# Loading image 1's first group-norm tile and the second layer's weights within the planned first steps of a conv/attention kernel

## Chip, cores, metric

One core of one Trainium2 chip. The metric is the device time of one execution in microseconds (us). Ratios are the mean time of one kernel's fast runs over that of the other's of the same rounds on the same chip, so they are not quite the ratio of the medians quoted beside them; the profiled execution stands outside the rounds.

## The reference, cut to what matters

`x` is four images of 64x64 positions and 96 channels. The first layer works on `_gn(x)`, a group norm whose mean and variance need a whole image before its first position can be normalised:

```python
def _gn(v, G=32, eps=1e-5):
    g = v.reshape(B_, H_, W_, G, C_ // G)
    m = jnp.mean(g, axis=(1, 2, 4), keepdims=True)
    s = jnp.var(g, axis=(1, 2, 4), keepdims=True)
    return ((g - m) / jnp.sqrt(s + eps)).reshape(v.shape)

def step(h, ins):                     # a scan over the 4096 positions of an image
    h_new = d * (A_t * h) + d * (B_t * u_t[..., None])
    y = g_t * jnp.sum(C_t * h_new, axis=-1)
```

A, B, C and d, u, g are projections of the normalised x. The second layer (linear attention and a quantised FFN) uses ten weight and bias arrays that are not needed before the first layer has got some way.

## The kernel before: the parts concerned

The sequence is cut into 32 chunks of 512 positions, 8 for each image, and a chunk into 12 steps; in step s, tile s (one of 12 parts of the state) is scanned. The engines run their instructions in the order in which the program writes them (in the trace the gx load, which waits for nothing, is issued at 59.12 us, just after a read-back that had waited 2.7 us). There are two ways of writing them:

- the first six steps come out of a small **list scheduler** (`Plan`). Each job has an engine, a cost, and jobs it comes after; the scheduler picks the job that can start first by its own estimate, calls its function, and so fixes the order;
- all later work hangs on step numbers: `at(step, fn)`. What is hung on steps below 6 is written right after the planned part.

```python
def load_gx(b, i):
    t = gxt[b, i] = sb("gx", [P, J, C], F32, f"gx_{b}_{i}")
    nc.sync.dma_start(t, gx_v[b, i])

def load_late():                       # ten loads, cut
    nc.sync.dma_start(w_o[0:C, :], w_out)
    ...
    nc.sync.dma_start(b2_sb, b2.partition_broadcast(P))

class GroupNorm:                       # sums for the images 1 to 3, on TensorE and ScalarE
    def first(self):
        self.transpose(0, "M", "gc")   # four transposes of gx[b, 0] on TensorE
        t = small.tile([C, 1], F32, tag="gc", name=f"gc_{self.b}", bufs=2)
        nc.scalar.activation(self.ps, self.ps, AF.Copy, accum_out=t)
        ...

def group_norm(b, s0):
    ...
    if b == 1:
        when = [8, 15, 22, 29, 36, 43, 50, 57]
    at(when[0] - 7, load_gx, b, 0)     # step 1: written after the planned part
    at(when[0] - 2, make)              # step 6: GroupNorm(b).first()

def planned_start():
    ...
    a = job("SP", 0.5, second.write, after=[a], late=3.4)   # d, d*u of chunk 1 to DRAM
    job("SP", 1.8, second.read, after=[a])                  # and back, spread over 128 partitions (rep)
    ...
    plan.run(stay_awake)               # stay_awake: a filler matmul in planned gaps of TensorE
    return second

second = planned_start()
at(7, load_late)
```

SyncE (SP in the code and in the profile) issues nearly all loads and stores, in program order; an issue that has to wait holds up all behind it.

## Time and profile before

| | kernel before |
|---|---|
| time, median of 3 runs | 1226.73 us (1226.67 to 1226.94) |
| profiled span | 1224.3 us |
| TensorE / VectorE / POOL / ScalarE busy | 95 / 92 / 85 / 66% |
| longest single wait of TensorE | 9.5 us, for gx of image 1 |

In the lines of the timelines the first column is the start in us from the span's start, the second the duration; a bracket at the end tells how long the engine was idle before and what ended that. The clock in the views by stage is the share of TensorE's full clock that was granted: 1.00 is all of it (called warm below), and well under that is called cold.

### The profile page before, as it was taken

The page shows a single profiled execution, that of the slowest core. Times are in us where ns is not written, and L with a number is a line of the kernel's source. Part 1 is how long each engine was busy: PE and PEld are TensorE (multiplying, and loading weights), DVE is VectorE, ACT ScalarE, POOL GpSimd, SP SyncE. Part 2 cuts the span into 40 slices and gives each one's busy share as a digit, 9 for nine tenths or more (in the row PEclk, how much of TensorE's full clock was granted, in tenths as well). Part 3 has the DMA queues.
Part 4 walks back from the last instruction along what each step waited for, and adds up shares of the span by engine and source line. Part 5 has one row for each costly group of instructions (what it writes and reads, how often), then busy time and mean ns, then how long its engine had stood idle before and what let it go on. Part 6 is the DMA issues. An engine that isn't in the chain of part 4 may idle for free. (4 is left out here: it accounts for less than half of the span.)

```text
span 1224.3 us, 19361 instructions
## 1 busy us (share of the span) xinstructions
PE 1163.5 (95%) x5965; PEld 880.7 (72%) x5965; DVE 1130.5 (92%) x2103; ACT 808.6 (66%) x1808; POOL 1037.5 (85%) x1183
## 2 busy tenths in 40 slices
PE   6879999999999999899999999999999999999985
PEld 5666777777777777677777777677777777777663
DVE  6869999999999999799999999899999999999884
ACT  3546555655555677677777777777677677767474
POOL 5768878998888898899998898999999899989654
PEclk8989999999999999999999999999999999999999
DMA  7476667667777776766787778577866677667221
GB/s 181 97 146 149 149 144 163 153 155 154 160 158 164 174 157 133 175 158 154 161 175 159 151 159 184 128 158 154 179 150 159 152 172 158 151 144 162 64 67 39
DMA packets 104289, 182.14 MB, mean 149 GB/s; under 512 B 42637, under 2 KB 50769, under 8 KB 104186
## 3 DMA queue, kind: packets, MB, share of 16 engines
q1 hardware_dynamic: 90060, 106.96, 36.1%
q0 software_dynamic: 13536, 73.93, 30.0%
q8 instruction: 47, 0.77, 0.3%
q14 instruction: 56, 0.46, 0.1%
q10 hardware_dynamic: 590, 0.02, 0.0%
HBM read 69.12 MB, written 24.77 MB: 77 GB/s over the span
## 5 line engine op out<-in xcount | busy, mean ns | idle before, releaser
L751 POOL TENSOR_TENSOR bu<-bu,rep 128x512 f32<-128x512 f32 x384 | 560.9, 1504 | 11.7 <-ACT state L777 6.5
L748 ACT ACTIVATE bu<-Bps,b_bac 128x512 f32<-128x512 f32 x384 | 264.1, 688 | 287.7 <-PE Bps L244 265.7
L767 DVE TENSOR_TENSOR_SCAN h<-Aps,state,bu 128x512 f32<-128x512 f32 x336 | 426.4, 1269 | 12.7 <-POOL bu L751 3.5
L760 DVE SCALAR_TENSOR_TENSOR Aps<-Aps,b_bac,rep 128x512 f32<-128x512 f32 x384 | 282.4, 735 | 37.5 <-PE Aps L244 37.0
L244 PE MATMUL Bps<-xs,w 128*128 128x512 f32 x768 | 268.0, 430 | 3.3 <-ACT bu L748 3.2
L244 PE MATMUL Aps<-xs,w 128*128 128x512 f32 x768 | 249.1, 405 | 11.2 <-DVE h L767 10.1
L800 POOL TENSOR_TENSOR ch<-ch,h 128x512 f32<-128x512 f32 x128 | 195.0, 1523 | 13.6 <-ACT ch L797 13.3
L244 PEld LDWEIGHTS Aps<-xs,w 128*128 128x128 f32 x768 | 138.3, 188 | 67.3 <-DVE h L767 39.2
L244 PEld LDWEIGHTS Bps<-xs,w 128*128 128x128 f32 x768 | 129.3, 190 | 45.9 <-issue 25.2
L244 PE MATMUL Aps<-xl,w 128*128 128x512 f32 x384 | 152.1, 396 | 0.0
L244 PE MATMUL Bps<-xl,w 128*128 128x512 f32 x384 | 151.8, 395 | 0.0
L244 PE MATMUL Dps<-xs,w 128*128 128x512 f32 x384 | 120.9, 396 | 0.0
L244 PE MATMUL Cps<-xs,w 128*128 128x512 f32 x384 | 120.6, 395 | 0.0
L806 POOL DMA_DIRECT2D ch<-ch x94 | 89.8, 955 | 16.5 <-DMA ch<-ch 13.6
L791 DVE SCALAR_TENSOR_TENSOR ch<-Cps,b_bac,h 128x512 f32<-128x512 f32 x128 | 95.0, 742 | 0.5 <-PE Cps L244 0.5
L791 DVE SCALAR_TENSOR_TENSOR ch<-Dps,b_bac,h 128x512 f32<-128x512 f32 x128 | 94.7, 740 | 0.3 <-PE Dps L244 0.2
L244 PEld LDWEIGHTS Bps<-xl,w 128*128 128x128 f32 x384 | 72.5, 189 | 17.5
L244 PEld LDWEIGHTS Dps<-xs,w 128*128 128x128 f32 x384 | 72.4, 188 | 17.6
L244 PEld LDWEIGHTS Aps<-xl,w 128*128 128x128 f32 x384 | 72.3, 188 | 17.6
L244 PEld LDWEIGHTS Cps<-xs,w 128*128 128x128 f32 x384 | 72.1, 188 | 17.5
L244 PE MATMUL Dps<-xl,w 128*128 128x512 f32 x192 | 75.7, 394 | 0.0
L244 PE MATMUL Cps<-xl,w 128*128 128x512 f32 x192 | 75.7, 394 | 0.0
(196 smaller groups left out, 2086.4 us busy)
## 6 DMA issues: line engine op xcount, KB each, us to landing
ch<-ch POOLq DMA_DIRECT2D x94, 768.0 KB, 6.5
rep<-ddd SPq DMA_DIRECT2D x124, 384.0 KB, 5.8
ddd<-dd SPq DMA_DIRECT2D x31, 384.0 KB, 3.0
xl<-lo SPq DMA_DIRECT2D x62, 128.0 KB, 2.4
x<-in_x_dram SPq DMA_DIRECT2D x32, 192.0 KB, 3.0
xatd<-xat SPq DMA_DIRECT2D x32, 192.0 KB, 3.1
xal<-xatd SPq DMA_DIRECT2D x32, 192.0 KB, 4.7
out_dram<-o SPq DMA_DIRECT2D x32, 192.0 KB, 2.8
```

What stands on the lines that cost most here:

```text
L244: nc.tensor.matmul(ps, lhsT=wt[:, n], rhs=mv, start=(n == 0), stop=(n == 2))
L748: nc.scalar.activation(self.bu, self.b_ps, AF.Identity, bias=self.bias(0))
L751: nc.gpsimd.tensor_tensor(self.bu, self.bu, rep[self.b, self.i][:, 1, self.cg], ALU.mult)
L760: nc.vector.scalar_tensor_tensor(self.a_ps, self.a_ps, self.bias(1), rep[self.b, self.i][:, 0, self.cg], ALU.add, ALU.mult,)
L767: nc.vector.tensor_tensor_scan(self.h, self.a_ps, self.bu, 0.0 if self.i == 0 else state[self.sh, self.cg], ALU.mult, ALU.add,)
L791: nc.vector.scalar_tensor_tensor(self.slot(), self.c_ps, self.bias(2), self.h, ALU.add, ALU.mult)
L800: nc.gpsimd.tensor_tensor(self.ch, self.ch, self.h, ALU.mult)
L806: nc.gpsimd.dma_start(chs[g, 0], chs.pop((g, sh)), accum_op=ALU.add)
```

## The change

The intent: both loads depend on nothing, so they can be jobs of the planned start. `land("free0", 34.0)` is a job of no engine that ends at planned time 34.0, so the gx load is placed once SyncE is free after that, and the ten late weights after 37.0.

```diff
         when = [s0 + SUMS + NT * n for n in range(NCH)]
         if b == 1:
             when = [8, 15, 22, 29, 36, 43, 50, 57]
-        at(when[0] - 7, load_gx, b, 0)
+        if b > 1:
+            at(when[0] - 7, load_gx, b, 0)
         at(when[0] - 2, make)
@@
         job("SP", 1.8, second.read, after=[a])
+        plan.rank = 4
+        job("SP", 0.5, load_gx, 1, 0, after=[land("free0", 34.0)])
+        job("SP", 4.0, load_late, after=[land("free1", 37.0)])
@@
     second = planned_start()
 
-    at(7, load_late)
```

## The prediction

> **What bounds the kernel now.** I read five views in this order: the page (engine shares), the waits of TensorE over the whole span, the waits of the DMA queue, the timelines of SyncE and TensorE around the wait found, and busy time by stage. The page says that the body is bound by work, with TensorE first and VectorE close behind it:
>
> ```profile
> PE 1163.5 (95%) x5965; PEld 880.7 (72%) x5965; DVE 1130.5 (92%) x2103; ACT 808.6 (66%) x1808; POOL 1037.5 (85%) x1183
> ```
>
> So an isolated TensorE stall early in the kernel costs its length, unless later slack swallows it, and five idle per cent of 1224.3 us are about 61 us. The TensorE waits show one single item that stands out:
>
> ```profile
> PE Aps L244 <- DVE h L767: 10.1, 26, 1.4
> PE gc_ps L481 <- DMA gx<-in_x_dram: 9.5, 1, 9.5
> PE gx_ps L481 <- DMA x<-in_x_dram: 4.8, 3, 3.7
> ```
>
> Columns: total us, times, longest us. The second line is one wait of 9.5 us, for the very tile that the change moves. The SyncE timeline (start us, duration us) shows why that tile comes late:
>
> ```profile
> 39.19 0.59 SPq L238 DMA_DIRECT2D w<-w  x1
> 47.01 0.57 SPq L632 DMA_DIRECT2D xs<-lo  x1
> ...
> 53.97 0.34 SPq L681 DMA_DIRECT2D ddd<-dd  x1
> 57.04 2.04 SPq L688 DMA_DIRECT2D rep<-ddd  x4
> 59.12 0.44 SPq L112 DMA_DIRECT2D gx<-in_x_dram  x1
> 59.61 0.43 SPq L217 DMA_DIRECT2D w_o<-in_L_conv_W_out_dram  x1
> ```
>
> The gx load depends on nothing, but it is written after the whole planned start, so it sits in SyncE's in-order queue behind the write of dd (waits for VectorE until 53.97) and its read-back (waits for that write until 57.04), and behind 4 x 384 KB of read-back in the DMA engines. The queue is idle from 39.78 to 47.01. On TensorE:
>
> ```profile
> 57.99 0.40 PE L244 MATMUL Cps<-xl,w 128*128 128x512 f32 x1
> 67.91 1.09 PE L481 MATMUL gc_ps<-ident,gx 128*96 128x128 f32 x4 [9.53 <-DMA gx<-in_x_dram]
> 68.65 1.20 PE L244 MATMUL Bps<-xs,w 128*128 128x512 f32 x2
> ```
>
> 9.53 us idle, then matmuls at about twice their usual duration. By stage (length, then busy us of PE, PEld, DVE, ACT, POOL; granted clock, DMA share, GB/s):
>
> ```profile
> 40.00:46.00 6.00, 5.89 (x27) 4.05 (x26) 5.69 (x7) 3.32 (x6) 3.88 (x3) 1.00 0.11 26
> 58.00:62.00 4.00, 0.38 (x2) 0.00 (x0) 1.95 (x3) 0.00 (x0) 3.26 (x5) 0.97 1.04 223
> 62.00:68.00 6.00, 0.09 (x1) 0.09 (x2) 0.00 (x0) 0.00 (x0) 0.00 (x0) 0.50 0.89 178
> 68.00:72.00 4.00, 4.00 (x12) 3.29 (x13) 0.40 (x1) 2.88 (x9) 1.33 (x2) 0.50 0.33 86
> ```
>
> From 62 to 68 no compute engine does anything to speak of: this is a stall of the whole core, not of TensorE alone. In 40 to 46, where the load would go, the DMA engines are nearly empty.
>
> **What the Trainium skill says.** (1) "TensorE: Matmul & The Clock Gate", Part 1 (What's actually happening): after an idle window of about 3.4 us TensorE falls to half its clock, and gets it back after some 3.4 us of sustained work. The trace agrees: 0.50 granted in 62 to 68 and still in 68 to 72. So the stall is paid twice. (2) "DMA: Bandwidth & Descriptors", Anatomy of one DMA: DMA engines do not wait on semaphores; a wait happens on the issuing sequencer before dispatch. The trace agrees: gx has no dependency, yet is issued at 59.12, just after a read-back that waited 2.7 us for its write. (3) Same page, Queues, rings and completion order: descriptors of one queue are consumed in ring order on each engine. The trace agrees roughly: gx, 192 KB, took 8.7 us behind the read-back, against 3.4 us for the quickest gx load of the same stretch.
>
> **The change, part by part.** It adds no instruction and removes none; it moves eleven issues (one gx, ten late weights) up SyncE's order.
>
> Where they land: I took the list schedule of the kernel before as written. It gives SyncE its last weight copy at planned time 31.38 to 32.38, then nothing until the write of dd at 48.18; the split of the second tile (which issues xs and xl) is planned at 40.94. A job released at 34 and one released at 37 that takes 4.0 therefore fall after all fourteen weight copies and before xs/xl. They have no successors and are on SyncE alone, so the order on the compute engines does not move.
>
> In real time the last copy ends at 39.78. gx is then issued at about 39.85 and lands at about 43 to 44 (3.4 us), some 14 us before TensorE wants it at 58.38. The ten late issues last 3.25 us in the timeline before (0.43, 0.33, 0.32, 0.23, 0.32, 0.23, 0.40, 0.32, 0.31, 0.36), with some 0.06 between them about 3.9 us: 40.3 to 44.2. VectorE has lo ready for xs only at 47.0, so the issue time is free. Their bytes (gx 192 KB, weights 36+108+36+144+144+48 KB, in all about 0.7 MB) at some 200 GB/s take 3.6 us and fall into the stretch that moved 26 GB/s. They should be gone by about 46 to 47.
>
> What goes away:
> - TensorE's wait: 67.91 - 9.53 = 58.38, so 9.53 us.
> - The cold clock. From 67.91 to 72.35 (start of the B matmuls after D) TensorE does four transposes and three groups of three matmuls. In the warm part of the same timeline a group takes 0.70 (72.35 to 73.04, 73.04 to 73.74) and four transposes 0.35 (74.44 to 74.79): 3 x 0.70 + 0.35 = 2.45 instead of 4.44. That is 2.0 us.
> - Sum: 11.5 us. Cross-check on VectorE: it idles 11.54 us before its next a_mul at 71.60, and would now start that at about 60.3, when the warm A group is done; 11.3 us.
>
> The ten late weights being early brings nothing by itself: their first user is at step 20, and no wait on them is in the list.
>
> What is given back: in the old stall the read-back of rep landed unseen. The SyncE timeline shows this: each late issue after 61 starts about 2 us after the last (61.15, 63.22, 65.14, 67.18), each released by a piece of rep, so the last piece landed at about 67.1. Tile 12 is its first user. Its multiply on POOL ran at 77.28; 11.3 earlier is 66.0. Without the 0.38 MB that shared the wire, rep would end about 1.8 us earlier (65.3); but POOL's first accumulating gather (768 KB, issued at 71.89) now comes at about 62.6 (POOL ends its two multiplies at 61.35, then one of 1.28), into the tail of rep. Halving the rate from about 63.5 puts rep at 67 to 68.5 and the gather at about 70. POOL would then wait 1 to 2 us for rep and 1 to 3 us before the second gather. Scan 12, at about 72.3, and a_mul 12, at about 70.3, come later than that, and POOL has 6.8 us of slack in the 37 us after 72. I book 0.5 us of net loss. 11.5 - 0.5 = 11.0 gives 1226.73 - 11.0 = 1215.7, a gain of 0.9%.
>
> **Rivals.**
> (a) *The read-back becomes the new wait.* Rep or the gathers land later than I estimate, and tile 12 stalls VectorE and TensorE by 2 to 4 us, some of it with a cold clock again. For it: the DMA engines are full (1.04) exactly there, and the work that used to fall in the quiet now falls on top. Against: 2 us and more of margin at a_mul 12. It would make 1218 to 1220.
> (b) *The gain is given back later*, since POOL, or a DMA-bound stage downstream, set the pace and the old stall only let it catch up. For: POOL is 85% busy, and there is a 2.8 us wait of TensorE for xl at 497. Against: TensorE has no wait over 0.7 us for 400 us after 72, and all that feeds it is issued by engines that move up with it. It would make 1220 to 1226.
> (c) *Early loads hurt the start*: late weights delay xs/xl, whose user at 50.85 has only some 0.3 us of margin (the last xl copy starts at 48.27 and takes 2.3). For: a tight margin. Against: an empty wire from 42 on. It costs 1 us at most: 1216.7.
> (d) *Luck in the phase of DMA*: the wait at 497 vanishes or grows, plus or minus 2.5.
>
> **Range and chances.** The centre is the mechanism with a small loss. The low end, 1213.2, is the full 11.5 and half of (d); the high end, 1219.0, is most of (a). A gain over 2% would take 24.5 us, more than twice what this stall holds; a loss over 2% would need a new stall of 36 us net of the gain. One per cent each.
>
> **What would show it.** In the changed kernel: SyncE issues gx at about 40 and the ten weights until about 44; the 9.5 us wait of TensorE for gx is gone; four transposes at about 58.4 take 0.6 us in a granted clock of 1.00 and not 1.09; TensorE's D group that began at 71.36 begins at about 60.1. At 100 us of the old time the same instruction is about 11 us earlier, and it stays so to the end. Wrong would be: a wait of over 2 us for rep near 66 to 72 (a), a lead that shrinks between 100 and 1150 (b), a wait for xl at 50.9 (c).

## The result and the profile after

The changed kernel took 1216.88 us (median of 4, 1215.26 to 1219.61) against 1226.84 us (median of 4, 1226.67 to 1227.2): ratio 0.9921, 95% interval 0.9899 to 0.9942. That is 10 us less, within 2%, and inside the predicted range. The predicted 1215.7 is a ratio of 0.9910, which lies in the interval too.

TensorE's waits over the whole span (total us, times, longest us), changed kernel, the top four; the one for gx is nowhere in the list:

```profile
PE Aps L244 <- DVE h L768: 10.3, 26, 1.4
PE y_ps L1036 <- ACT hq L1030: 4.4, 5, 2.0
PE xnt_ps L619 <- DVE z L379: 4.1, 4, 2.0
PE dug_ps L244 <- DMA xl<-lo: 3.6, 2, 2.7
```

SyncE's timeline, changed kernel: gx and the ten weights are issued after the last weight copy and are done 3.6 us before xs is issued. The read-back (`rep`) now has nothing behind it:

```profile
39.99 0.59 SPq L238 DMA_DIRECT2D w<-w  x1
40.63 0.59 SPq L112 DMA_DIRECT2D gx<-in_x_dram  x1
41.27 0.43 SPq L217 DMA_DIRECT2D w_o<-in_L_conv_W_out_dram  x1
...
45.06 0.36 SPq L226 DMA_DIRECT2D b_sb<-in_L_ffn_b_dram  x1
49.00 0.58 SPq L633 DMA_DIRECT2D xs<-lo  x1
...
55.97 0.34 SPq L682 DMA_DIRECT2D ddd<-dd  x1
59.03 1.77 SPq L689 DMA_DIRECT2D rep<-ddd  x4
```

This gx landed 2.6 us after its issue, against 8.7 us before. TensorE's timeline, changed kernel: the transposes follow the C matmuls at once and take 0.60 us (1.09 before):

```profile
60.00 0.40 PE L244 MATMUL Cps<-xl,w 128*128 128x512 f32 x1
60.23 0.60 PE L481 MATMUL gc_ps<-ident,gx 128*96 128x128 f32 x4
60.59 0.71 PE L244 MATMUL Bps<-xs,w 128*128 128x512 f32 x2
```

But they start at 60.23 and not, as predicted, at 58.4. Everything in this execution is 1.9 us late, well ahead of the changed instructions: the first projection started at 34.16 (32.18 before). That is a matter of the start, taken up below. A second profile of the same kernel (after_again) had an early start. Its stages (length, busy us of PE, PEld, DVE, ACT, POOL, granted clock, DMA share, GB/s) answer to those of the prediction:

```profile
40.00:46.00 6.00, 5.90 (x26) 4.06 (x26) 5.69 (x7) 3.18 (x6) 3.86 (x3) 1.00 0.56 146
58.00:62.00 4.00, 3.89 (x20) 2.83 (x19) 3.68 (x6) 2.91 (x9) 3.92 (x6) 1.00 0.91 211
62.00:68.00 6.00, 6.00 (x32) 4.87 (x31) 6.00 (x8) 4.10 (x13) 5.29 (x5) 1.00 1.10 222
68.00:72.00 4.00, 4.00 (x19) 3.16 (x18) 3.20 (x4) 3.16 (x8) 1.80 (x3) 1.00 0.38 97
```

TensorE and VectorE work through 62 to 68 without a gap, where nothing worked before, with DMA engines that are fuller than they were (1.10 against 0.89), and the clock is 1.00 throughout.

**Where the lead goes.** To follow it I took the start of the output projection of each of the 32 chunks (one per chunk, on TensorE) in each profile, and subtracted it from that of the first profile of the kernel before. Chunk 0's is at 103 us, chunk 31's at 1153:

```
chunk          0      4      8      9     11     12     16     24     31
after        9.17   9.28   9.30   9.32   9.34   7.86   7.85   8.07   8.05
after_again 11.06  11.07  11.09  10.14  10.14   9.90   9.84   9.81   9.77
after_third  9.20   9.38   9.45   8.67   8.71   5.65   5.68   5.72   5.77
before_again 0.39   0.44   0.50   0.52   0.49  -1.39  -1.45  -1.33  -1.38
```

Between the jumps the lead is constant to about 0.3 us over hundreds of us. The jumps are at two places. Between chunks 11 and 12 TensorE waits 2.7 to 3.2 us for a copy of xl in all five profiles, those of before included. The kernel before, profiled twice, jumps there by 1.9 us against itself. What differs is less the wait than the clock behind it. The stages just after that wait (same columns as above) in before (wait 2.79 us), after (2.70) and after_third (3.15):

```profile
497.00:501.00 4.00, 3.88 (x19) 2.97 (x20) 1.60 (x3) 2.23 (x5) 3.91 (x4) 1.00 0.82 183
488.00:492.00 4.00, 4.00 (x14) 3.28 (x13) 0.52 (x2) 1.60 (x4) 4.00 (x5) 0.58 0.84 180
489.00:493.00 4.00, 4.00 (x12) 3.18 (x12) 0.06 (x1) 1.34 (x4) 4.00 (x5) 0.50 0.86 178
```

The clock stayed at 1.00 in before, after_again (wait 3.05 us), gx_only and gx_between, and fell in after, after_third, before_again, late_only, gx_act and gx_wire; these six are the ones that lose 1.3 to 3.1 us there against the first profile of before. So this jump is again a cold clock behind a wait, met in some executions and not in others, and the first profile of before, to which all leads refer, is one that escaped it. The smaller jump, between chunks 8 and 9, is a wait of TensorE for a sum on POOL (1.6 us in after_again, 1.4 in after_third, 0.4 in after, none in before), which came late since POOL had waited some 2 us for a gather. The differences at the end are the lead won at 58 to 72 us, plus the start and these two places.

### The profile page after: what moved, and what is told of

The parts are those of the page before.

```text
span 1216.6 us, 19359 instructions
## 1 busy us (share of the span) xinstructions
PE 1165.7 (96%) x5965; PEld 882.2 (73%) x5965; DVE 1131.5 (93%) x2103; ACT 808.7 (66%) x1808; POOL 1037.4 (85%) x1183
```

## Experiments

Eleven runs in three calls (three of them repeat a kernel unaltered); those of one call share their runs of the kernel before (medians 1227.15, 1226.31 and 1227.65). The question was which part of the move does the work, how the 11.5 us divide, and where the spread comes from.

### after_again and after_third: the changed kernel, unaltered

> The changed kernel once more, unaltered. Its four runs were 1215.26, 1215.48, 1218.29 and 1219.61 us and the profiled one (1218.29) reached the gx transposes 1.85 us late, of which about 1 us is a late release of the TensorE clock between 28 and 36 us. Theory S (start-up luck[...]): runs spread again between about 1215 and 1220, and a profile of a run near 1215.3 has its gx transposes at 58.2 to 58.6 us. Theory D (DMA luck in the middle: the wait for xl near 490 us): the gx transposes are always near 58.4 or 60.2 and the spread comes from a wait for xl that is 1.5 us longer in slow runs.

> The changed kernel once more on this chip, as the partner of warm_start and gx_between: 1215 to 1220 us. Its lead over the kernel before, tile by tile, should again be constant within 0.1 us but for the same two or three places where a wait for a DMA differs (tiles 8 to 9 and 11 to 12 of the 32).

Measured: 1217.07 us (1215.22 to 1218.94), ratio 0.9919 (0.9902 to 0.9937); and 1216.29 us (1215.64 to 1220.71), ratio 0.9914 (0.9900 to 0.9927). On these chips the kernel before spread as well (1224.92 to 1232.37 in eleven runs), so the narrow 0.5 us of its first four runs had been luck. Both theories have their part. Starts: the first projection is at 34.16, 32.31 and 34.13 us in the three profiles, which is the 1.9 us between their leads at chunk 0. DMA: at chunk 12 after_third (1220.71 us) loses another 3.1 us. Its wait for xl is 3.2 us, but that is only 0.4 longer than in the first profile of before; most of the loss is the cold clock behind it.

### gx_only, late_only: one half of the move each

```diff
# gx_only: the changed kernel, but
-        job("SP", 4.0, load_late, after=[land("free1", 37.0)])
+    at(7, load_late)
# late_only: the changed kernel, but
-        job("SP", 0.5, load_gx, 1, 0, after=[land("free0", 34.0)])
-        if b > 1:
-            at(when[0] - 7, load_gx, b, 0)
+        at(when[0] - 7, load_gx, b, 0)
```

> Only the gx load is moved into the first steps; the ten late weight loads stay at step 7. Theory (the gx move alone carries the gain): 1215 to 1219 us, equal to the changed kernel within its spread, with no wait for gx on TensorE, though the SP queue stays blocked by the read-back until about 67 us. Rival (the late weights in the wire hinder the read-back of rep and the second gx load, so both moves are needed): 2 us and more slower than the changed kernel, with a wait for rep or gx between 65 and 80 us.

> Only the ten late weight loads are moved; gx is loaded at its old place behind the read-back. Theory: the wait of TensorE for gx stays, shortened by at most the 1.8 us that the late weights held the wire: 1225 to 1227 us, wait 7.7 to 9.5 us. Rival (the wire, not the order, made gx late): the wait falls to about 5 us or less and the time to about 1222.

Measured: gx_only 1216.46 us, ratio 0.9918 (0.9899 to 0.9937); late_only 1227.11 us, ratio 1.0002 (0.9984 to 1.0021). The gx move alone carries the gain; the weights alone are worth nothing. The wait in late_only fell from 9.5 to 8.2 us, within the 1.8 us estimated for the wire that the weights had taken. But it was 9.1 and 8.7 us in two further profiles with the weights at their old place (before_again, warm_before), so the weights' own share is not settled:

```profile
PE gc_ps L481 <- DMA gx<-in_x_dram: 8.2, 1, 8.2
```

The rival of gx_only is not quite dead: its lead at chunk 0 is 9.76 us with a start as early as after_again's (gx transposes at 58.43 and 58.36), so 1.3 us less. POOL's timeline of gx_only points to the late weights, still in the way behind the read-back:

```profile
67.33 1.29 POOL L752 TENSOR_TENSOR bu<-bu,rep 128x512 f32<-128x512 f32 x1 [0.92 <-DMA w_ff<-in_L_attn_Wff_dram]
72.20 0.89 POOL L807 DMA_DIRECT2D ch<-ch  x1 [3.58 <-DMA ch<-ch]
```

And of after_again:

```profile
67.05 1.29 POOL L752 TENSOR_TENSOR bu<-bu,rep 128x512 f32<-128x512 f32 x1 [0.71 <-DVE ch L792]
70.54 0.89 POOL L807 DMA_DIRECT2D ch<-ch  x1 [2.19 <-DVE h L768]
```

The second gather waits 3.58 us instead of 2.19 (the last line names VectorE; but the second gather is issued 0.6 us after the first has landed in both runs, at 69.9 and 71.6 us, so I take the first gather for what it waited for), and xs of chunk 2 lands late, with a TensorE wait of 0.7 us for it near 79 us. The other profiles bear this out. From the D group behind the gx transposes to chunk 0, the three with the weights late and no stall (gx_only, gx_between, gx_act) lose 1.3, 1.0 and 0.8 us of lead; the four with the weights early (after, after_again, after_third, warm_start) lose 0.1. So moving the weights as well is worth about 1 us in the traces up to there. The run times cannot tell it: 0.9918 lies among 0.9914 to 0.9921 of the changed kernel. One possible reason, not shown: the loss between chunks 8 and 9 (0.8 to 1.2 us) came in three of the five profiles with the weights early and in none of the eight with them late.

### gx_between: ahead of the read-back, but not early

```diff
-        a = job("SP", 0.5, second.write, after=[a], late=3.4)
+        def write_and_gx():
+            second.write()
+            load_gx(1, 0)
+
+        a = job("SP", 0.5, write_and_gx, after=[a], late=3.4)
```

(The kernel before, with its later gx load of image 1 taken out and the weights left at step 7.)

> The kernel before, with the gx load put between the write of dd and its read-back in SyncE's queue: issued at about 54.4 us instead of 59.1, with the late weights left at step 7. Theory (it need only be ahead of the read-back, not in the first steps): gx lands at about 57.5, just ahead of its use at 58.4; no wait on TensorE; 1215 to 1219 us, the same as the changed kernel. Rival (gx beside the write of dd delays that write, so the read-back and tile 12 come later): the read-back starts over 1 us later than 57.04, and 1 to 3 us of the gain are lost.

Measured: 1216.54 us (1216.16 to 1217.37), ratio 0.9918 (0.9905 to 0.9932). gx was issued at 55.22, with the write of dd, and TensorE did not wait for it at 59.08. So the place in the queue that matters is ahead of the read-back. The read-back starts 1.5 us later than 57.04, as the rival had it, but 0.9 of that is the later start of this execution; write to read-back took 3.67 us (54.83 to 58.50), against 3.07 before (53.97 to 57.04). So the rival's cost is about 0.6 us at that place.

### gx_act and gx_wire: another queue

```diff
# both: the kernel before, but
-        nc.sync.dma_start(t, gx_v[b, i])
+        (nc.scalar if (b, i) == (1, 0) else nc.sync).dma_start(t, gx_v[b, i])
# gx_wire also: in step 6 and not in step 1
-        at(when[0] - 7, load_gx, b, 0)
+        at(when[0] - (2 if b == 1 else 7), load_gx, b, 0)
```

> The kernel before, with only one thing altered: the gx load keeps its place in the program (right after the planned start) but is issued by ScalarE's DMA queue instead of SyncE's. ScalarE is free at about 57.9 us. Theory (half of the lateness is the wire: rep's 1.5 MB is in flight from 57.6 on): gx is issued at about 58, lands at 60.5 to 63 us, TensorE waits 2.5 to 4.5 us instead of 9.5, and the time is 1218 to 1221 us. Rival Q (only the queue order matters): it lands some 3 us after its issue, wait about 2.5 us, time about 1217.5 to 1218.5. Rival W (only the wire matters): it still lands at 66 to 68 us and the time stays at 1225 or more.

Measured: 1216.93 us (1215.26 to 1219.37), ratio 0.9922 (0.9907 to 0.9937). I had misjudged where ScalarE stands: it issued gx at 54.02, before the read-back (55.16 in this early start), and TensorE waited 0.35 us. The run shows once more that it is enough to issue gx ahead of the read-back, but says nothing of the wire. Hence:

> The run gx_act missed its purpose: ScalarE issued gx at 54.0 us, before the read-back (55.2), so the load never met a full wire. Here gx is again issued by ScalarE's DMA queue, but in step 6, just before the transposes, behind the last state copy (57.67 to 57.85 us in the kernel before), while the read-back is issued from 57.04 on. Theory (half of the lateness is the wire): issued at about 57.9 of the kernel before's time, lands 4 to 6 us later, TensorE waits 3.5 to 5.5 us, and the clock falls little or not; 1218.5 to 1221.5 us. Rival Q (only the queue order): lands 3 us after issue, TensorE waits 2.5 us, 1217 to 1218.5 us. Rival W (only the wire): lands 8 us and more after issue, 1224 us or more.

Measured: 1221.31 us (1220.40 to 1223.25), ratio 0.9955 (0.9937 to 0.9973). Timeline and stage of gx_wire:

```profile
57.74 2.03 SPq L688 DMA_DIRECT2D rep<-ddd  x4
57.82 0.36 ACTq L112 DMA_DIRECT2D gx<-in_x_dram  x1
...
62.61 1.09 PE L481 MATMUL gc_ps<-ident,gx 128*96 128x128 f32 x4 [3.54 <-DMA gx<-in_x_dram]
```

```profile
62.00:66.00 4.00, 3.39 (x11) 2.85 (x12) 0.00 (x0) 2.18 (x7) 0.67 (x2) 0.57 1.07 219
```

Issued with the read-back, gx can be used by TensorE 4.8 us later: 2.2 us more than the 2.6 us on a quiet wire, and 3.9 us less than behind the read-back in SyncE's own queue. So the full wire counts. How much of the 3.9 us the queue itself is worth is not shown: gx was issued here 0.1 us after the first of the read-back's four pieces, and not after the last as in the kernel before, so it also had fewer bytes ahead of it, whatever the queue. One thing I had wrong: I expected little or no loss of clock after a wait of 3.5 us. It fell to 0.57, and the transposes took 1.09 us as after the long stall.

### warm_stall: the stall without the cold clock

```diff
+        if b == 1:
+            def keep_warm():
+                ps = bank("M", [P, TC], "keep_warm")
+                for _ in range(36):
+                    nc.tensor.matmul(ps, lhsT=w_dug[:, 0, 0:P], rhs=w_bac[0][:, 0, 0],
+                                     start=True, stop=True)
+            at(when[0] - 2, keep_warm)
         at(when[0] - 2, make)
```

> The kernel before with 36 matmuls without use (128x512) put on TensorE ahead of the gx transposes, so that it works through the stall and keeps its clock. They should take about 36 x 0.233 = 8.4 us, a little less than the stall of 9.5. Theory (2.0 us of the loss is the cold clock after the stall): the transposes start at about 67.9 as before, the granted clock in 68 to 72 us is 1.00 and not 0.50, and the time is 1224.7 us. Rival (the cold clock is hidden, since VectorE or POOL would pace the steps after the stall anyway): the clock is 1.00 and the time stays at 1226.5 or above.

Measured: 1223.85 us (1222.15 to 1224.89), ratio 0.9973 (0.9956 to 0.9990). Timeline and stages of warm_stall:

```profile
58.69 8.56 PE L585 MATMUL keep_warm<-w,w_dug 128*128 128x512 f32 x36
68.23 0.61 PE L481 MATMUL gc_ps<-ident,gx 128*96 128x128 f32 x4 [0.97 <-DMA gx<-in_x_dram]
```

```profile
62.00:68.00 6.00, 5.26 (x23) 3.90 (x21) 0.00 (x0) 0.00 (x0) 0.00 (x0) 1.00 0.92 190
68.00:72.00 4.00, 3.72 (x17) 2.85 (x18) 1.72 (x3) 3.09 (x9) 1.55 (x2) 1.00 0.32 86
```

The stall is still there (VectorE, ScalarE and POOL do nothing in 62 to 68), the clock is 1.00. The D group starts at 70.08 and not at 71.36, although gx came 0.32 us later: 1.6 us in this profile, of the 2.0 predicted. The runs give 3.3 us with an interval of 1.2 to 5.4, so they confirm that the kernel became faster, not by how much to better than that. In the profile only 1.2 us of the lead are there at chunk 0; another 1.8 us come at chunk 12, by a shorter wait for xl, far from the place that was changed. The rival, that other engines would have paced those steps anyway, falls: the 1.2 us are kept.

### warm_start and warm_before: the clock at the start

The spread pointed at the fillers of the planned start. 28 filler matmuls stand before the first projection. In the profile of the changed kernel:

```profile
28.49 5.92 PE L1247 MATMUL awake<-ident 128*128 128x128 f32 x28
34.16 0.70 PE L244 MATMUL wide_ps<-xs,w_rep 128*128 128x512 f32 x2
```

VectorE had ended the first projection's input at 32.7 us; the fillers held it up to 34.16, at a clock of 0.50. In before they took 4.92 us. The suspect for the cold clock was the four us ahead of them, where TensorE waits before each of four short transposes. In before, that stretch and the next look like this:

```profile
24.00:28.00 4.00, 1.56 (x7) 1.02 (x8) 4.00 (x6) 0.67 (x2) 3.23 (x4) 0.95 0.52 122
28.00:32.00 4.00, 4.00 (x25) 4.00 (x24) 3.89 (x14) 3.97 (x6) 2.09 (x5) 0.62 0.41 98
```

So I filled those waits, in the changed kernel (warm_start) and in the kernel before (warm_before):

```diff
-        a = mm(0.5, first.transpose, after=[a], key="M:x")
+        def transpose_awake():
+            first.ps = bank("M", [C, TC], f"xnt_ps_{first.nm}")
+            for j in range(J):
+                for _ in range(4 if j else 8):
+                    stay_awake()
+                nc.tensor.transpose(first.ps[:, j * P : (j + 1) * P], first.t[:, j, :], ident)
+
+        a = mm(0.5, transpose_awake, after=[a], key="M:x")
```

> The changed kernel with 20 filler matmuls (128x128) put among the four transposes of the first tile, between 22 and 28 us, where TensorE waits 0.6 to 2 us before each and its clock falls. The planned 28 fillers after them took 3.29 us in a run with a warm clock, 4.92 to 5.92 in runs with a cold one, and where they are slow they hold up the first projection. Theory S (the cold clock here is a large part of the spread and of a mean loss): the 28 fillers take about 3.3 to 3.6 us, the first projection waits for VectorE's xl instead of the fillers, the time falls 0.5 to 1.5 us below the changed kernel's and the spread narrows. Rival (start-up spread comes from the arrival of the x loads and VectorE's slow multiplies): the fillers are faster but time and spread stay.

> The kernel before, with the 20 fillers of warm_start and the gx load at its old place. If the gain of warm_start (2.7 us by the ratios 0.9892 and 0.9914) belongs to the start alone and adds to that of the gx load, this kernel is 2 to 3 us faster than the kernel before (ratio about 0.998) and its spread is within 2 us. Rival (it was luck, or comes from the interplay with the earlier gx load): ratio 0.9995 to 1.0005, or a spread as wide as the kernel before's.

Measured: warm_start 1213.25 us (1212.72 to 1214.63), ratio 0.9892 (0.9879 to 0.9906): the fastest of all, 1.1% under the kernel before. warm_before 1224.08 us (1223.46 to 1226.66), ratio 0.9979 (0.9965 to 0.9993). So the fillers are worth about 2.6 us with and without the gx move, by ratios that are each good to some 1.7 us; within that, the two gains add. Timeline of warm_start:

```profile
27.70 3.29 PE L1254 MATMUL awake<-ident 128*128 128x128 f32 x28
30.75 0.70 PE L244 MATMUL wide_ps<-xs,w_rep 128*128 128x512 f32 x2
32.05 0.50 PE L244 MATMUL wide_ps<-xl,w_rep 128*128 128x512 f32 x1 [0.60 <-DVE xl L658]
```

The 28 fillers take 3.29 us and the projection waits for VectorE's xl, as theory S said; the clock is 1.00 from 24 to 36 us. What stays open is where the 2.6 us come from. At chunk 0 warm_start leads by 11.57 us, 0.5 more than after_again with its good start and 2.4 more than the two profiles with a poor one; a further 1.8 us come at chunk 12, by a shorter wait for xl (1.0 us). And the profile of warm_before (1226.66, the slowest of its five runs) is 0.6 us behind the first profile of before at chunk 0 and gains 2.0 us at chunk 12, with a wait of 0.9 us. The only other profile with a clock of 1.00 from 24 to 32 us, warm_stall, waits 1.0 us there too; the ten with a cold clock at the start wait 2.0 to 3.2. So the short wait may belong to the warm start and not to luck, but how is not shown. The narrower spread was seen in warm_start's four runs (1.9 us) and not in warm_before's five (3.2 us). By the spans of the core, which leave out what lies before the first and after the last instruction, the spreads are 0.5 and 1.8 us, against 2.9 and 3.2 us for the kernel before: the slowest run of each, the profiled one, spent 3.6 and 3.2 us outside the span, the others 1.7 to 1.9.

### before_again: a second profile of the kernel before

> The kernel before once more, for a second profile of it: the wait for gx on TensorE should again be 9 to 10 us with the granted clock at 0.5 behind it, whatever the start does; its tiles should differ from the first profile by a constant, but for the places where a wait for a DMA differs.

One look, 1227.41 us. The wait for gx is 9.1 us, the clock 0.50 in 62 to 68 and 0.56 in 68 to 72, as expected. Its line in the table above is what showed that the jump at chunk 12 belongs to neither kernel: here the clock fell behind the wait for xl (0.50 from 499 to 501 us), and in the first profile it did not.

## Why the prediction was right

- **The stall, 9.53 us.** Right. The wait was 9.1 and 8.7 us in two further profiles that have it (before_again, warm_before), so the profile that was read had a long one. It is gone in every profile of the changed kernel, and a move of gx alone gives the same time as the whole change.
- **The cold clock, 2.0 us.** Right in kind; warm_stall shows 1.6 us in its profile. Comparing D group with D group, before (71.36) and after_again (60.20, with transposes at 58.36 for a predicted 58.38), the two terms together are 11.16 us, for 11.5 predicted.
- **The order and the loads' places.** Right: after all weight copies, issued by 45.4 us at the latest, before xs. gx landed 2.6 us after its issue, for 3.4 predicted. With the early start of after_again xs, xl and the write of dd stand within 0.15 us of before, so rival (c) falls.
- **"The ten late weights being early brings nothing by itself."** Right as it stands (late_only: ratio 1.0002), but incomplete: with the stall gone they would lie in the wire against tile 12 and the second gather, and leaving them there costs some 1 us of lead up to chunk 0 in three traces. I had booked their absence from the wire only as 1.8 us of earlier rep.
- **Net loss 0.5 us, rival (a).** The second gather was to wait 1 to 3 us and waited 2.19. POOL's multiply for tile 12 was predicted 1 to 2 us after 66.0 and came at 67.05, but POOL stood idle only 0.71 us before it (0.2 us or less in after and after_third) and the profile names VectorE for it, so the predicted wait of 1 to 2 us for rep is not seen. Neither stopped VectorE or TensorE: in after_again TensorE has one wait over 0.5 us up to 96 us, the 0.6 us for ScalarE that stood at 95.89 in the kernel before. The loss up to chunk 0 is 11.16 - 11.06 = 0.1 us.
- **Rival (b), given back later.** Not seen as a slow loss: the lead is flat between the jumps. The jump between chunks 8 and 9 (about 0.8 to 1 us in two of three profiles of the changed kernel, 1.2 us in late_only, none in the second profile of before) is of the kind of (b), though: TensorE waits for POOL, and POOL for a gather. And one reading behind "Against" was wrong: TensorE does have a wait over 0.7 us in the 400 us after 72, 1.33 us for ScalarE at 155.33.
- **What I had not foreseen: the spread.** The times before (three runs within 0.27 us) had let me leave the start out. The three sets of the changed kernel gained 9.7 to 10.5 us by their ratios, for 11.0 predicted. That is within the intervals; whether the missing 0.5 to 1.3 us is more than the start and the clock behind the xl wait is open. Rival (d) had put down the wait at 497 as luck in the phase of DMA, plus or minus 2.5 us; the size fits (jumps of -3.1 to +2.0 us at chunk 12), the cause is in good part the clock. The median held with 2 us to spare on the slow side, which had been put there for rival (a), but one of the four runs (1219.61) lay above 1219.0: that the number hit is sound, that it hit so closely is in part luck.
- **A sum that was wrong.** The low end, "the full 11.5 and half of (d)", is 1226.73 - 11.5 - 1.25 = 1214.0 and not 1213.2.

## What to carry to other kernels

A load that depends on nothing still waits for all that stands ahead of it in an in-order queue; look for it by the longest single wait of the busiest engine, and put it ahead of the next issue that waits or moves much. The stall was paid again in the cold clock behind it (1.6 us), and a stretch of short waits can cost clock too, so filling both with idle matmuls is a cheap test and sometimes a gain. A wait of 2.5 to 3.2 us cost the clock in six executions and not in three others: before an effect is put down to the length of a wait, look at the granted clock behind it. When a gain is smaller than what is predicted, align the two traces by a repeated instruction: a constant lead with jumps tells apart what was won at the change from what came elsewhere; profile the old kernel twice, since its one profile can be the lucky one.

## What the Trainium skill lacked or had wrong

- "DMA: Bandwidth & Descriptors", Issuing engines are not separate DMA queues: it says that starting DMAs on several engines only saves the sequencer's time for starting them. No run here shows it wrong. What it lacks is how much the moment and place of the issue can be worth: the same 192 KB landed 2.6 us after issue on a quiet wire, 7.9 to 8.7 us after it behind a 1.5 MB read-back in SyncE's queue, and could be used 4.8 us after it when ScalarE issued it just behind the read-back's first piece (gx_wire). By that page's section Queues, rings and completion order, an engine takes turns between queue rows packet by packet; gx_wire fits that but does not show it.
- "TensorE: Matmul & The Clock Gate", Why this matters for your kernels: its rule is no idle gaps over about 3 us. A single gap of 3.54 us did cost the clock (0.57 granted in 62 to 66 us of gx_wire), which agrees. But near 3 us the rule does not decide: a gap of 2.70 us cost the clock (0.58 in the 4 us behind it, after) and one of 3.05 us did not (1.00, after_again).
- The same page also tells of short idle times between groups of matmuls that make the clock go back and forth in another kernel, but gives no busy share. Here a chain of waits of 0.64, 0.76, 0.82 and 1.49 us at four short transposes (TensorE busy 1.56 of 4 us, before) was followed by a clock of 0.62 in the next 4 us; with 2.17 of 4 us busy it was followed by 1.00 (warm_stall), and filling the waits held it at 1.00 (warm_start).
- That page says that the cold start varies from run to run; no page gives what this does to the spread of whole-kernel times. Here the first projection moved between 32.3 and 34.2 us from one execution of the changed kernel to the next: 0.8 us of that stood before the fillers, 1.0 us came by slower fillers. The shift stayed in the lead through chunk 8.
